# One table of expert slots for all four batches, filled in two passes, in a fused block of attention, mixture of experts and rotation

## The chip, the cores and the metric

The kernel runs on one core of one Trainium2 chip, in float32. Times are microseconds (us) of one execution on the device. A time without further words is the median of several runs; the profile is of one execution.

## The reference

Four batches of 512 tokens with 288 channels go through a block with adaptive layer norms, a mixture of experts, and then a rotation of a 64-dimensional subspace. Cut to what matters:

```python
mod = silu(c) @ w_adaln + b_adaln             # 6 vectors of 288 for each batch
h = ln(x) * (1 + sc_msa) + sh_msa
q, k, v = heads(h @ w_qkv + b_qkv)            # 16 heads of 18
o = softmax(q k^T * 18 ** -0.5) v
x = x + g_msa * (o @ w_proj + b_proj)
xn = ln(x) * (1 + sc_mlp) + sh_mlp            # 2048 tokens
logits = xn @ w_gate                          # 4 experts
gates = softmax(top2(logits))
eo[e] = gelu_tanh(xn @ w1[e] + b1[e]) @ w2[e] + b2[e]     # 288 -> 1152 -> 288
x = x + g_mlp * sum_e(gate[e] * eo[e])        # for a token's two experts
U, _ = qr(P)                                  # P is 288 x 64
R = expm(skew(silu(c) @ W.T + b))             # 64 x 64 for each batch
out = x + ((x U) R - x U) U^T
```

With two experts for each token there are 4096 rows of expert work. From the reference's inputs, the rows of the four experts are 229, 226, 337, 232 in batch 0; 193, 284, 265, 282 in batch 1; 177, 265, 297, 285 in batch 2; 249, 262, 281, 232 in batch 3.

## The kernel before

The whole order of instructions on each engine is written out by hand: the program is traced in the order in which its pieces are called, and no scheduler moves anything. All of it is in `fast_path`; another path, `general_path`, follows behind a flag and runs only if some expert gets more rows than its slots.

**Attention (to 270.6 us).** The work is cut into 32 pairs, eight for each batch (`HALF`): groups of four heads by pairs of token tiles. In a pair TensorE computes scores (`z`, L1905), ScalarE their exponentials (`es`, L1914, two for each group), and TensorE multiplies them with the values (`av`, L1925, in `gather`). The list `plan` places all other pieces into slots of the pairs, called a, s and b: projections of the next batch (`pq`, L1827; `pv`, L1790), the output projection of the batch before (`merges`, `po`, L1999), its routing (`choose`), columns of a Householder QR on VectorE (`column`, L1617 to L1693, one after another, 64 in all), the squarings of the matrix exponential (`square`, `psq`, L1514), the clearing of tables, and scatters (`scatter_next`, one indirect DMA on GpSimd for each tile of 128 tokens and each of its two choices, L2275). Normalized tiles `xh` are made by ScalarE (only batch 0's first norm by VectorE), transposed by TensorE and modulated into `hT` (L1250, L1256).

**Tables.** Batches are handled in two halves of two. In each half the experts are ranked by their rows, and rank r has `CAPS[r]` slots, in a table `slots0` or `slots1` of 2304 rows of 296 values: 288 channels, four weights and four places, each by rank. A row is scattered to its slot by its rank within its expert (`ranks_of`, pc L2155 to L2169, then `slots_of`). The sums go to `chosen0` and `chosen1`.

**Experts (270.6 to 630.2 us).** For each half and rank, eight times in all, i = 0 to 7:

- `hidden(i)`: 9 blocks f, taken by twos. For each block, matmuls of `w1s` (L2648) and of the last 32 channels from `w1r` (L2661) with the transposed slots `xgT` into `ph`; then ScalarE's gelu into `hm` (L2670).
- `outputs(i)`: tiles of 128 slots. For each, 18 matmuls into `pe` (L2708), a weighted sum `y`, and an indirect DMA on GpSimd that adds the rows to `chosen` (L2725). Each of these DMAs waits until the one before it has landed.
- Ranks 1 and 2 have 576 slots, which is four tiles and a half; their two halves form one shared tile, whose rows are in `xgS` and `hmS`, and which belongs to rank 2's outputs.
- `load_slots(i + 1)` (on SP; for i = 0 on GpSimd, during attention) and its transposes (`pt`, L2406, copied to `xgT` by ScalarE, L2407) lie between them, and the weights of the next expert are loaded on SP (`expert_weights`).

A list `rest` gives one more piece to each of 108 steps (72 blocks and 36 tiles): batch 2's routing, batch 3's merges and routing, the remaining columns, and at its end `ends`: the basis chain from `pwt` (L1698) over `pg`, `pnt`, `pN` and `pR` (L1725 to L1729) to `pY`, `pU` and `pu`, with the loads and additions of the first batches' sums beside it.

**Finish (630.2 us to the end).** `Finish` takes pairs of token tiles in turn: transposes (`pxT`, L2784), `pz` (L2795), `py` (L2810), an addition on VectorE (L2818) and a store (L2820).

The slots of a half in the kernel before:

```python
CAPS = (640, 576, 576, 512)
FIRST = (0, 640, 1216, 1792)
SLOTS = 2304
ROW = 288 + 2 * 4
```

Of the kernel before, what the change touches and what calls it, by code (L numbers as in the profile page):

```python
# [10 lines left out]
F32 = mybir.dt.float32  # L11
# [17 lines left out]
CAPS = (640, 576, 576, 512)  # L29
FIRST = (0, 640, 1216, 1792)  # L30
SLOTS = 2304
ROW = 288 + 2 * 4
# [3 lines left out]
WARM = 6  # L36
# [794 lines left out]
def fast_path(  # L831
# [76 lines left out]

    slots = [dram.tile([SLOTS, ROW], F32, name=f"slots{h}") for h in range(HALVES)]

    chosen = [
        dram.tile([B * N // HALVES, C], F32, name=f"chosen{h}")
        for h in range(HALVES)
    ]
# [3 lines left out]
    brow = [const.tile([P, E + 1], I32, name=f"brow{h}") for h in range(HALVES)]  # L918
    b1r = const.tile([P, HALVES, E, NF], F32, name="b1r")
    numbers, wxs = {}, []  # L920

    def expert_weights(i):
# [4 lines left out]
        h, r = divmod(i, E)  # L927
# [48 lines left out]
    with ExitStack() as s1:  # L976
# [78 lines left out]
        def compact(item, copy):  # L1055
            w = wqk[:CC, :, item, :].rearrange("p k (h d) -> p k h d", d=HD)
            for at, i, h, n in parts_of(item):
                heads = raws[int(h >= HS)].rearrange("p k t (h r) -> p k t h r", r=HQ)
                copy(w[:, :, ds(at, n), :], heads[:, :, i, ds(h - HS * (h >= HS), n), :HD])
            w = wqk[CC : CC + 1, 0, item, :].rearrange("o (h d) -> o h d", d=HD)  # L1060
            b = braw.rearrange("o (c r t g) -> o t g c r", c=4, t=2, g=NG)
            for at, i, g, c, n in in_groups(item):
                copy(w[:, ds(at, n), :], b[:, i, g, ds(c, n), :HD])
# [107 lines left out]
        bounds = const.tile([P, 2, E, E], F32, name="bounds")  # L1171
# [3 lines left out]
        for e in range(E):  # L1175
            nc.gpsimd.memset(bounds[:, 0, :, e : e + 1], float(FIRST[e]))
            nc.gpsimd.memset(bounds[:, 1, :, e : e + 1], float(FIRST[e] + CAPS[e]))
            nc.gpsimd.memset(expert[:, :, e : e + 1], float(e))
            nc.gpsimd.memset(ranks[:, e, :], float(e))
            nc.gpsimd.memset(tie[:, e : e + 1], float(E - 1 - e))  # L1180

        tokeni = const.tile([P, TT // HALVES], I32, name="tokeni")
        nc.gpsimd.iota(
            tokeni, pattern=[[P, TT // HALVES]], base=0, channel_multiplier=1
        )
        token = const.tile([P, TT // HALVES], F32, name="token")
# [6 lines left out]
        nc.gpsimd.memset(empty[:, :C], 0.0)  # L1193
        nc.gpsimd.memset(empty[:, C:], 1.0e6)
# [16 lines left out]

        def spreads_of(b, which, mv):
# [3 lines left out]
            if (b, which) != (0, 0):  # L1216
# [7 lines left out]
        def normalized(b, which, mv, rs):  # L1224

            xh = rt.tile([P, NT, C], F32, tag="xh", name=f"xh{which}{b}", bufs=2)
            for t in range(NT):
                if (b, which) != (0, 0):
# [4 lines left out]
                        bias=mv[:, t : t + 1],  # L1233
# [31 lines left out]
        def clear_slots():  # L1265
            def clear(h, i):
                nc.gpsimd.dma_start(out=slots[h][ts(i, P), :], in_=empty)

            def clear_sums(h, i):
                nc.sync.dma_start(  # L1270
                    out=chosen[h][ds(i * 4 * P, 4 * P), :].rearrange("(t p) c -> p t c", p=P),
                    in_=empty[:, :C].unsqueeze(1).to_broadcast([P, 4, C]),
                )

            return [
                lambda h=h, i=i: clear(h, i)
                for h in range(HALVES)
                for i in range(SLOTS // P)
            ] + [
                lambda h=h, i=i: clear_sums(h, i)  # L1280
                for h in range(HALVES)
                for i in range(B * N // HALVES // (4 * P))
            ]
# [66 lines left out]
        def skew_matrices(between):  # L1350
# [51 lines left out]
            def stores(part):  # L1402
                for at, (r, to, i, lo, n) in enumerate(runs[part::8]):
# [9 lines left out]
            def last():  # L1413
# [25 lines left out]
                + [lambda part=part: stores(part) for part in range(8)]  # L1439
                + [load]  # L1440
                + idle * 2
# [3 lines left out]
        def rotations():  # L1445
# [124 lines left out]
            def last():  # L1570
# [8 lines left out]
                + [lambda k=k: square(k) for k in range(SQUARINGS_FAST)]  # L1579
# [353 lines left out]
        def normalize(n):  # L1933
# [18 lines left out]
            def first():  # L1952
# [7 lines left out]
                for c, k, at in placed:  # L1960
                    (nc.gpsimd if n == NN - 1 else nc.sync).dma_start(out=chunk(oTs, k, "oc")[at, :], in_=oraw[ds(c * HQ, HD), :])
# [90 lines left out]
        TH = BH * NT  # L2052
        halves = {}
        scatters = []
        scattered = [[] for _ in range(HALVES)]
# [5 lines left out]
        def choose(b, xr):  # L2061

            h, b1 = divmod(b, BH)
            tiles = ds(b1 * NT, NT)
            if b1 == 0:
                halves[h] = (

                    small.tile([P, 2, TH, E], F32, tag="kk", name=f"kk{h}", bufs=2),  # L2070

                    small.tile([P, TH, 2, E], F32, tag="raw", name=f"raw{h}", bufs=2),

                    small.tile([P, TH, E], F32, tag="both", name=f"both{h}", bufs=2),
                    small.tile([P, TH + 1, E], F32, tag="sums", name=f"sums{h}", bufs=2),
                    [],
                )
            kk, raw, both, sums, xrs = halves[h]
            xrs.append(xr)
            k1, k2 = kk[:, 0, tiles, :], kk[:, 1, tiles, :]  # L2080
# [42 lines left out]
            def choices():  # L2123
                nc.vector.tensor_add(both[:, tiles, :], k1, k2)
                if b1 == 0:
                    nc.vector.memset(sums[:, 0, :], 0.0)
                for t in range(b1 * NT, (b1 + 1) * NT):
                    nc.vector.tensor_add(sums[:, t + 1, :], sums[:, t, :], both[:, t, :])

                nc.vector.tensor_copy(  # L2130
                    raw[:, tiles, 1, :],
                    token[:, tiles].unsqueeze(2).to_broadcast([P, NT, E]),
                )

            def gates_of():
# [6 lines left out]
                cb = raw[:, tiles, 0, :]  # L2142
# [8 lines left out]
            def ranks_of():  # L2151

                pc = bank([P, N], f"pc{h}")
                pn = pc[:, TH * E : (TH + 1) * E]
                nc.tensor.matmul(  # L2155
                    pc[:, : TH * E],
# [6 lines left out]
                    pc[:, : TH * E],  # L2163
                    every,
                    sums[:, :TH, :].rearrange("p t e -> p (t e)"),
# [3 lines left out]
                nc.tensor.matmul(pn, every, sums[:, TH, :], start=True, stop=True)  # L2169

                def square(name):
                    return small.tile([P, E, E], F32, tag=name, name=f"{name}{h}", bufs=1)


                pos = small.tile([P, TH + 1, E], F32, tag="pos", name=f"pos{h}", bufs=1)
                nc.vector.tensor_copy(
                    pos.rearrange("p t e -> p (t e)"), pc[:, : (TH + 1) * E]
                )
                size = small.tile([P, E], F32, tag="size", name=f"size{h}", bufs=1)
                nc.vector.scalar_tensor_tensor(  # L2180
                    size, pos[:, TH, :], float(E), tie, ALU.mult, ALU.add
# [10 lines left out]
                has = square("has")  # L2192
# [6 lines left out]
                for half in range(2):  # L2199
                    part = ts(half, P // 2)  # L2200
                    nc.vector.tensor_copy(
                        number[part, E : E + 1], number[part, half + 1 : half + 2]
                    )
                nc.vector.tensor_copy(brow[h], number)
                ends_ = small.tile([P, 2, E, E], F32, tag="ends", name=f"ends{h}", bufs=1)
                nc.vector.tensor_tensor(
                    ends_,
                    bounds,
                    has.rearrange("p r e -> p e r").unsqueeze(1).to_broadcast([P, 2, E, E]),
                    ALU.mult,  # L2210
                )
                first_last = small.tile([P, 2, E], F32, tag="fl", name=f"fl{h}", bufs=1)
                nc.vector.tensor_reduce(first_last, ends_, AX.X, ALU.add)
                nc.vector.tensor_copy(lastslot[:, h], first_last[:, 1])
                nc.vector.tensor_add(nextslot[:, h], first_last[:, 0], pos[:, TH, :])
                kept.extend((pos, has, first_last[:, 0]))

            def by_rank():

                has = kept[2]  # L2220
                of = small.tile([P, TH * 2, E, E], F32, tag="of", name=f"of{h}", bufs=1)
                nc.vector.tensor_tensor(
                    of,
                    raw.rearrange("p t k e -> p (t k) e")
                    .unsqueeze(2)
                    .to_broadcast([P, TH * 2, E, E]),
                    has.unsqueeze(1).to_broadcast([P, TH * 2, E, E]),
                    ALU.mult,
                )
                for i, xr_ in enumerate(xrs):  # L2230
                    nc.vector.tensor_reduce(
                        xr_[:, :, C:],
                        of[:, ds(i * NT * 2, NT * 2)].rearrange(
                            "p (t k) r e -> p t (k r) e", k=2
                        ),
                        AX.X,
                        ALU.add,
                    )
# [6 lines left out]
                    has.unsqueeze(2).to_broadcast([P, E, NF, E]),  # L2245
# [4 lines left out]
            def slots_of():  # L2250
                pos, _, firsts = kept[1:]
                pos = pos[:, :TH, :]

                def all_(m):
                    return m.unsqueeze(1).to_broadcast([P, TH, E])

                nc.vector.tensor_tensor(pos, pos, all_(firsts), ALU.add)

# [785 lines left out]
```

## Time and profile before

| | |
|---|---|
| runs of the kernel before | 659.48, 659.94, 659.95 us; median 659.94 |
| the profiled execution's own time | 658.79 us |
| its span (first to last instruction) | 657.1 us |
| granted TensorE clock | 0.996 of full speed |
| TensorE (PE) busy | 644.2 us, 98% |
| VectorE (DVE) busy | 440.9 us, 67% |
| ScalarE (ACT) busy | 293.7 us, 45% |
| GpSimd (POOL) busy | 267.1 us, 41% |

The expert stage in the profile begins at these times (us), hidden(i) first and then outputs(i):

| i | 0 | 1 | 2 | 3 | 4 | 5 | 6 | 7 |
|---|---|---|---|---|---|---|---|---|
| hidden | 270.6 | 324.4 | 366.4 | 411.4 | 451.1 | 498.4 | 539.8 | 587.2 |
| outputs | 299.4 | 346.8 | 387.9 | 431.1 | 474.8 | 520.2 | 561.3 | 612.7 |

How to read the views: the page's busy tenths cut the span into 40 slices, one digit each. The chain goes back from the last instruction to what released each, and is told in order of time as start, duration, engine, tile and line, with the number of instructions in a run. The timeline tells the same for one engine, with `[idle before <-releaser]` where the engine had stood idle. A matmul's end is modelled, so a group's duration is a little longer than its share of the engine, and periods are read from starts.

### The profile page before, as it was taken

The page shows a single profiled execution, that of the slowest core. Times are in us where ns is not written, and L with a number is a line of the kernel's source. Part 1 is how long each engine was busy: PE and PEld are TensorE (multiplying, and loading weights), DVE is VectorE, ACT ScalarE, POOL GpSimd, SP SyncE. Part 2 cuts the span into 40 slices and gives each one's busy share as a digit, 9 for nine tenths or more (in the row PEclk, how much of TensorE's full clock was granted, in tenths as well). Part 3 has the DMA queues.
Part 4 walks back from the last instruction along what each step waited for, and adds up shares of the span by engine and source line. Part 5 has one row for each costly group of instructions (what it writes and reads, how often), then busy time and mean ns, then how long its engine had stood idle before and what let it go on. Part 6 is the DMA issues. An engine that isn't in the chain of part 4 may idle for free.

```text
span 657.1 us, 11381 instructions
## 1 busy us (share of the span) xinstructions
PE 644.2 (98%) x3558; PEld 380.9 (58%) x3558; DVE 440.9 (67%) x1989; ACT 293.7 (45%) x469; POOL 267.1 (41%) x392
## 2 busy tenths in 40 slices
PE   7999999999999999999999999999999999999995
PEld 3534344443444344567767767776677676776763
DVE  5545757796667137582989988888888898342125
ACT  4468557775686557743343232232323322312232
POOL 4034589754352766503505745314043042251120
PEclk9999999999999999999999999999999999999998
DMA  8549333232323644366416642665064353551044
GB/s 211 117 149 231 111 87 94 81 110 73 106 72 86 196 137 112 118 178 181 76 16 208 141 156 38 160 181 91 17 173 82 92 126 58 135 123 34 10 84 159
DMA packets 77364, 75.74 MB, mean 115 GB/s; under 512 B 35168, under 2 KB 67437, under 8 KB 77294
## 3 DMA queue, kind: packets, MB, share of 16 engines
q1 hardware_dynamic: 62106, 47.88, 26.6%
q0 software_dynamic: 14784, 26.62, 17.6%
q8 instruction: 30, 0.49, 0.3%
q10 hardware_dynamic: 404, 0.42, 0.3%
q14 instruction: 40, 0.33, 0.2%
HBM read 47.68 MB, written 20.88 MB: 104 GB/s over the span
## 4 chain that ended last, share of the span: by engine, by line
PE 88%; DMA 5%; DVE 3%; SPq 2%; ACT 1%; issue 1%; DVEq 0%; ACTq 0%
PE pe L2708 24%; PE ph L2648 22%; PE z L1905 9%; PE av L1925 7%; PE pq L1827 6%; PE ph L2661 4%; PE po L1999 4%; PE pv L1790 3%; PE pt L2406 2%; DMA raw<-in_w_qk_dram 1%; PE pz L2795 1%; PE pxT L2784 1%; DMA qk<-row 1%; DMA rdr<-den 1%; DVE pl L2088 1%; PE py L2810 1%
## 5 line engine op out<-in xcount | busy, mean ns | idle before, releaser
L2708 PE MATMUL pe<-w2s,hm 128*128 128x288 f32 (+1 forms) x648 | 163.7, 408 | 0.0
L1914 ACT ACTIVATE es<-z 128x1024 f32<-128x1024 f32 x128 | 126.3, 1023 | 64.3 <-PE z L1905 62.2
L2648 PE MATMUL ph<-xgT,w1s 128*128 128x288 f32 (+2 forms) x576 | 151.7, 413 | 0.4
L2708 PEld LDWEIGHTS pe<-w2s,hm 128*128 128x128 f32 (+1 forms) x648 | 118.7, 187 | 31.8 <-issue 2.3
L2648 PEld LDWEIGHTS ph<-xgT,w1s 128*128 128x128 f32 x576 | 105.8, 190 | 40.6 <-issue 11.9
L2670 ACT ACTIVATE hm<-ph,b1r 128x576 f32<-128x576 f32 (+2 forms) x72 | 49.9, 738 | 122.0 <-PE ph L2661 122.0
L2725 POOL DMA_INDIRECT chosen<-y,place x38 | 61.0, 1604 | 69.4 <-DMA chosen<-y,place 36.9
L1905 PE MATMUL z<-qk 32*128 32x512 f32 x512 | 78.4, 639 | 0.2 <-DMA qk<-row 0.2
L2723 POOL TENSOR_TENSOR y<-y,gb 128x288 f32<-128x288 f32 x32 | 27.9, 872 | 115.6 <-ACT y L2722 115.6
L2722 ACT ACTIVATE y<-pe,weight 128x288 f32<-128x288 f32 x32 | 16.0, 501 | 107.3 <-PE pe L2708 107.3
L1925 PE MATMUL av<-es,vt 128*32 128x512 f32 x512 | 61.7, 598 | 0.0
L1827 PE MATMUL pq<-hT,wqk 96*126 96x512 f32 (+4 forms) x156 | 59.0, 510 | 1.2 <-ACT hT L1256 1.2
L1827 PEld LDWEIGHTS pq<-hT,wqk 97*126 97x126 f32 (+3 forms) x156 | 25.5, 178 | 38.3 <-issue 30.1
L2275 POOL DMA_INDIRECT slots<-xr,where x32 | 32.5, 1014 | 35.1 <-DVE where L2272 21.1
L1646 DVE STREAM_SHUFFLE wj<-pt 32x288 f32<-32x288 f32 (+47 forms) x96 | 42.2, 439 | 0.6
L1905 PEld LDWEIGHTS z<-qk 32*128 32x128 f32 x512 | 23.5, 182 | 26.8 <-ACT es L1914 16.8
L1925 PEld LDWEIGHTS av<-es,vt 128*32 128x32 f32 x512 | 13.5, 109 | 42.8 <-issue 42.8
L1874 POOL DMA_DIRECT2D qk<-row x42 | 21.2, 510 | 40.8 <-ACT row L1869 30.8
L1620 DVE SCALAR_TENSOR_TENSOR pt<-wj,uf,pt 64x288 f32<-64x288 f32 (+62 forms) x63 | 34.5, 548 | 2.2
L1635 DVE SCALAR_TENSOR_TENSOR q<-q 64x1 f32<-64x1 f32 (+1 forms) x128 | 31.0, 242 | 4.6
L1617 DVE SCALAR_TENSOR_TENSOR prf<-pt,q,wj 64x288 f32<-64x288 f32 (+62 forms) x63 | 31.6, 501 | 2.2
L2661 PE MATMUL ph<-xgT,w1r 32*128 32x288 f32 (+2 forms) x288 | 30.6, 453 | 0.0
(286 smaller groups left out, 826.6 us busy)
## 6 DMA issues: line engine op xcount, KB each, us to landing
w2s<-in_w_dram SPq DMA_DIRECT2D x8, 1296.0 KB
w1s<-in_w_dram SPq DMA_DIRECT2D x8, 1152.0 KB
slots<-empty POOLq DMA_DIRECT2D x36, 148.0 KB, 3.2
qk<-row POOLq DMA_DIRECT2D x42, 72.0 KB, 3.3
spread<-rdr SPq DMA_DIRECT2D x64, 36.0 KB
chosen<-empty SPq DMA_DIRECT2D x4, 576.0 KB
out_dram<-xs SPq DMA_DIRECT2D x8, 288.0 KB
wr<-in_wrT_dram POOLq DMA_DIRECT2D x4, 567.0 KB, 5.2
```

The source lines that it names most:

```text
L1620: nc.vector.scalar_tensor_tensor(m, w, u[rows, :], m, ALU.mult, ALU.add)
L1646: nc.vector.stream_shuffle(wj[o : o + HQ, j:], pt[o0 : o0 + HQ, j:], [j % HQ] * HQ)
L1827: nc.tensor.matmul(pq[:n, at], wqk[:rows, k, item, :n], hT[:rows, k, at], start=start, stop=(k == NK - 1),)
L1905: nc.tensor.matmul(zs[c // 2][:, c % 2, :], qk[ts(c, HQ), 1, ts(t, P)], qk[ts(c, HQ), 0, :], start=True, stop=True,)
L1914: nc.scalar.activation(e, z, AF.Exp, scale=SCALE)
L1925: nc.tensor.matmul(avs[n][ts(c, HQ), :], vts[b % 2][:, t, ds((4 * g + c) * (HD + 1), HQ)], es[c // 2][:, c % 2, :], start=(t == 0), stop=( ...
L2275: made = nc.gpsimd.indirect_dma_start(out=slots[h], out_offset=bass.IndirectOffsetOnAxis(ap=where[:, i, t : t + 1], axis=0), in_=xrs[t // ...
L2648: nc.tensor.matmul(ph[:, j, :SB], w1s[:, k, ts(f, P)], xgT[:, k, ts(j, SB)], start=(k == 0), stop=False,)
L2661: nc.tensor.matmul(ph[:, j, :SB], w1r[rows, f0 // 2, :], xgT[rows, 2, ts(j, SB)], start=False, stop=True,)
L2670: nc.scalar.activation(hm[:, f, : CAPS[r]].rearrange("p (j s) -> p j s", j=NB), ph[:, :, :SB], AF.Gelu_apprx_tanh, bias=b1r[:, h, r, f : f ...
L2708: nc.tensor.matmul(po[ts(m, rows), :], slots_[:, f, :], w[:, f, :], start=(f == 0), stop=(f == NF - 1),)
L2725: nc.gpsimd.indirect_dma_start(out=chosen[h], out_offset=bass.IndirectOffsetOnAxis(ap=place[:, t + m : t + m + 1], axis=0), in_=y, in_offs ...
```

## The change

- There is one table `slots` with 1280 rows for each expert, of 293 values (288 channels, four weights by expert, one place), and one `chosen`. Positions run on over all four batches. The first pass is ranked after batches 0 and 1 and has 640, 576, 544 and 512 slots; rows of batch 2 fill what is free in it, except for the biggest expert, whose batch-2 rows begin at its 640th slot. The second pass takes what is left, with 640, 576, 448 and 512 slots, where the third expert worked on is rank 3 (448) and the fourth is rank 2 (512). By the counts above the second pass has 578, 493, 455 and 336 rows.
- `load_slots` starts at rows read into registers, with two DMAs in place of six; GpSimd then copies the last 32 channels three times more (`copies`) and picks the weights (`ends`). The second expert's load is issued behind the first hidden layer and waits for batch 2's scatters.
- There are 35 output tiles in place of 36.
- Batch 2's normalized tiles are made by VectorE. Its norm, logits and choices move from the first hidden layer into pairs 29 to 31, its last two merges share pair 28, and three columns leave the attention stage for the expert stage.
- The tables are cleared from pair 6 on, `chosen` in eight DMAs of 288 KB, each behind a reciprocal of batches 1 to 3 (it was four of 576 KB). The skew matrices are stored in seven parts, and `square(0)` gets a step without work behind it.
- At the front there is one warm-up group fewer, two of batch 0's normalized tiles are made by ScalarE, and the second half of the query and key weights is compacted by VectorE.
- At the end the basis chain takes the last 13 of 111 steps, from the last hidden layer on; an output tile of the last expert counts as two steps. The check of the flag comes behind it, and the last store is two of one tile each.

The core of the diff:

```diff
-CAPS = (640, 576, 576, 512)
-FIRST = (0, 640, 1216, 1792)
-SLOTS = 2304
-ROW = 288 + 2 * 4
+CAPS = ((640, 576, 544, 512), (640, 576, 448, 512))
+ORDER = ((0, 1, 2, 3), (0, 1, 3, 2))
+STRIDE = 1280
+SLOTS = 4 * STRIDE
+ROW = 288 + 4 + 1
...
-WARM = 6
+WARM = 5
...
+        PLAIN = ((0, 0), (B - 2, 1))
...
-                if (b, which) != (0, 0):
+                if (b, which) not in PLAIN or (b == 0 and t >= NT // 2):
                     nc.scalar.activation(
...
-            def clear_sums(h, i):
+            def clear_sums(i):
                 nc.sync.dma_start(
-                    out=chosen[h][ds(i * 4 * P, 4 * P), :].rearrange("(t p) c -> p t c", p=P),
-                    in_=empty[:, :C].unsqueeze(1).to_broadcast([P, 4, C]),
+                    out=chosen[ds(i * 2 * P, 2 * P), :].rearrange("(t p) c -> p t c", p=P),
+                    in_=empty[:, :C].unsqueeze(1).to_broadcast([P, 2, C]),
...
+                at = begun[:, b] if b else firsts
+                nc.vector.tensor_tensor(
+                    pos,
+                    pc[:, : (NT + 1) * E].rearrange("p (t e) -> p t e", e=E),
+                    at.unsqueeze(1).to_broadcast([P, NT + 1, E]),
+                    ALU.add,
+                )
...
+            load(xg[:, :n], ds(at, n * P), lambda m: m.rearrange("(t p) c -> p t c", p=P))
...
+            def copies():
+                nc.gpsimd.tensor_copy(
+                    xg[:, :n, C : 3 * P].rearrange("p t (g c) -> p t g c", c=HQ),
+                    xg[:, :n, 2 * P : C].unsqueeze(2).to_broadcast([P, n, 3, HQ]),
                 )
...
+            if n >= NG:
+                clear(1, 1)
...
                     for t, piece in enumerate(merges):
-                        also(at + 2 + t, "s", piece)
+                        also(at + 2 + min(t, 2), "s", piece)
                     routes[b - 1] = routing(b - 1)
+                    also(at + 5, "s", routes[b - 1][0])
+                    also(at + 5, "b", routes[b - 1][1])
+                    also(at + 6, "s", routes[b - 1][2])
+                    also(at + 7, "s", routes[b - 1][3], routes[b - 1][4])
...
-            SB = CAPS[r] // NB
+            SB = CAPS[h][u] // NB
...
-                for t in range(5 if r == 0 else 4)
+                for t in range(own_tiles(h, u))
...
+                    if f == NF // 2 and i + 1 == HALVES * E:
+                        yield
...
+            if not i:
+
+                takes = take_slots(1, load_slots(1, hp, "xg", 1))
```

## The prediction

> **What bounds the kernel now.** I read the page first: engine totals, the busy tenths, and the chain that ended last. Then came the chain entry by entry, and the timelines of the places that the diff touches.
>
> ```profile
> PE 644.2 (98%) x3558; PEld 380.9 (58%) x3558; DVE 440.9 (67%) x1989; ACT 293.7 (45%) x469; POOL 267.1 (41%) x392
> PE   7999999999999999999999999999999999999995
> DVE  5545757796667137582989988888888898342125
> ...
> PE 88%; DMA 5%; DVE 3%; SPq 2%; ACT 1%; issue 1%; DVEq 0%; ACTq 0%
> ```
>
> TensorE is busy for 644.2 of 657.1 us and full in every slice but the first and the last. VectorE is at 80 to 90% in the expert stage until 562.9 us. So TensorE work that goes away is time won, unless another engine is then late for it; VectorE is the nearest.
>
> **The change part by part.** The profiled execution took 658.79 us (span 657.1), 1.15 below the median of the runs, 659.94. The sum is made on the profiled one.
>
> *Narrower hidden layers.* Two blocks f of the hidden layer are 16 matmuls against w1s, and repeat as the chain shows:
>
> ```profile
> 375.54 4.08 PE ph L2648 x16
> 380.32 4.08 PE ph L2648 x16
> ...
> 415.70 3.65 PE ph L2648 x16
> 419.99 3.65 PE ph L2648 x16
> ...
> 461.17 4.50 PE ph L2648 x16
> 466.42 4.50 PE ph L2648 x16
> ```
>
> The periods are 4.78 us for 576 slots, 4.29 for 512, 5.25 for 640, so about 0.48 us for every 64 slots. A layer has 4.5 such steps, so 64 slots cost 2.15 us. The cap goes from 576 to 544 in the first pass (-1.08) and from 576 to 448 in the second (-4.30): -5.4. Below 512 slots no row shows a period. With no gain there it would be -3.2; I take the line: 3.65 us over 16 is 0.228 for 256 columns, the line gives 0.20 for 224, and the weight loads beside these matmuls take 0.19 each by the page.
>
> *One output tile and one transposed tile fewer.*
>
> ```profile
> 612.72 17.66 PE pe L2708 x72
> ```
>
> Four tiles of 18 matmuls take 17.66 us, so a tile takes 4.42. The second pass's third layer has four tiles in place of five: -4.4. The transposes of a tile and their wait are worth 0.3: -0.3.
>
> *Positions for two more batches.* They are worked once for each batch, no longer once for two: four groups of matmuls in place of two, each like the one from 208.82 to 209.51 us (pc), 0.69: +1.4.
>
> *The end of attention.* Batch 2's merges now lie in pairs 26, 27, 28 and 28, no longer in 29, and its routing in 29 to 31.
>
> ```profile
> 254.02 1.51 PE L1905 MATMUL z<-qk 32*128 32x512 f32 x8
> 255.46 1.73 PE L1999 MATMUL po<-wpg,oc 108*128 108x288 f32 x6
> ```
>
> Pairs 28 to 31 take 6.14, 6.20, 6.14 and 4.2 us. With two merges pair 28 should take 6.0 + 1.66 = 7.66; 29 and 30 are held near 6.1 by ScalarE's two 1.02-us exponentials for each group of scores and can't shrink; pair 31, with batch 2's logits, 4.9: +2.1 (0 if the po hides in waits for the exponentials, +3 if the logits wait for VectorE's norm, four passes of about 0.4 us). The routing leaves a first hidden layer in which TensorE never waits (28.80 us busy of 28.80) and is about 1 us of its work there; that small gain is left in the range.
>
> *Slot loads.* Two DMAs in place of six, then copies by GpSimd. The first load starts behind batch 2's rs at about 255.4 us, after a register load; landing about 262 and the copies 1 to 1.3 us (nearest row: a 576-element GpSimd copy, 0.70), against a need at 266: hidden, with 3 us to spare, and 1 us for each one that it is late. The later loads sit on SP behind the same releases as before, with the weights of the next expert behind them. Transposed tiles are placed earlier in the output layers: copies that were bare in two places and are now bare in one other: +0.5.
>
> *Clearing in smaller pieces.* At 234.26 TensorE waits 0.88 us for XY, which stands on VectorE behind the spread of reciprocals, whose DMA queues on SP behind a 576-KB clear of `chosen`:
>
> ```profile
> 210.26 5.25 DMA chosen<-empty
> ...
> 234.26 0.68 PE L1514 MATMUL psq<-XY 64*64 64x64 f32 x16 [0.88 <-DVE XY L1568]
> ```
>
> The clears become eight of 288 KB, each behind a reciprocal's own DMAs, and square gets an idle step: -0.9 (0 if a clear falls elsewhere in the way). The four more `slots` clears are on GpSimd's queue in attention and hidden.
>
> *Front.*
>
> ```profile
> 12.62 0.51 ACT L1059 COPY wqk<-raw 96x378 f32<-96x378 f32 x1 [1.18 <-DMA raw<-in_w_qk_dram]
> ...
> 13.67 2.11 ACT L1256 ACTIVATE hT<-pt,modT 96x512 f32<-96x512 f32 x3
> ...
> 14.59 5.39 PE L1827 MATMUL pq<-hT,wqk 97*126 97x512 f32 x12 [1.22 <-ACT hT L1256]
> ```
>
> hT stands on ScalarE behind the compaction of the second weight half. That copy goes to VectorE, its biases to GpSimd, one warm-up group goes away, and ScalarE gets two normalized tiles earlier, while it is idle. pq should start near 13.4: -1.2 (0 if the weights, which land at 12.60, then wait for VectorE).
>
> *End.* The basis chain, from pwt to pU, moves from the last two layers into the second half of the last hidden layer and the last output layer; each of its steps has 8 to 10 matmuls (1.96 to 2.4 us) over a VectorE answer of 0.28 to 0.71 us. The last store becomes two of one tile: -0.5 (0 to -0.8, half a tile pair of VectorE and half a transfer).
>
> Sum: -5.4 - 4.4 - 0.3 + 1.4 + 2.1 + 0.5 - 0.9 - 1.2 - 0.5 = -8.7 us. Span 648.4, profiled time 650.1, median about 651.3.
>
> **The rivals.** First, *VectorE's column chain becomes the bound*. The 64 columns of the QR are worked one after another on VectorE, and TensorE needs the last at pwt.
>
> ```profile
> 346.88 0.45 DVE L1646 STREAM_SHUFFLE wj<-pt 32x269 f32<-32x269 f32 x1
> ...
> 558.59 0.40 DVE L1646 STREAM_SHUFFLE wj<-pt 32x225 f32<-32x225 f32 x1
> ...
> 566.10 0.37 PE L1698 MATMUL pwt<-ident,pt 64*96 64x64 f32 x3
> ```
>
> The chain ended at 562.9, 3 us ahead of pwt. The twelve columns from 346.88 to 411.82 average 5.41 us, the 33 after them 4.58. The change takes three columns out of attention, so 48 remain, from about 350.5: 15 x 5.41 + 33 x 4.58 = 232.3, ending at 582.8. The last hidden layer began at 587.2 and begins 10.2 earlier (the sum without the last store, -8.2, and 2 us of chain that move behind it), at 577.0; pwt stands two periods (8.6) and half a step (2.0) into it, so at about 587.6. That leaves 5 us. For: GpSimd gets seven copies and some thirty small products in this stage, and VectorE's small steps do stretch beside it:
>
> ```profile
> 273.19 0.62 DVE L1678 SCALAR_TENSOR_TENSOR kap<-q 64x1 f32<-64x1 f32 x1
> 273.84 0.72 DVE L1681 TENSOR_TENSOR q<-kap,behind 64x1 f32<-64x1 f32 x1
> ...
> 273.71 2.52 POOL L1994 TENSOR_TENSOR wpg<-wp,gates 108x288 f32<-108x288 f32 x3
> ```
>
> Both usually take 0.15 us. Against: seven times 1.3 us plus thirty times 0.1 is 12 us, of which VectorE loses perhaps a third, 4 us, just inside the 5. [...] Worked from the rows alone: 1 us is lost for each us after 587.6. With late columns at 4.85 the end is 591.7, +4.1, and the median 655.4. It gets slower than before when the late columns average over 5.0; at 5.05 (+0.47 x 33 = 15.5 us) the end is 598.3, 10.7 late, and the median 662.
>
> Second, *batch 2's scatters hold the second expert's load*. Its rows now lie in the first pass, so the load waits for eight more scatters at about 1.6 us each after batch 2's positions at about 281, and lands near 305, needed at 317. GpSimd's queue also holds the products and copies there. If it lands late, each us is lost, and the weights behind it on SP (needed at 324) follow. 5 us late gives about 656.
>
> Third, *less gain*: no gain below 512 slots, +3 at the end of attention, no gain at the front: -8.7 + 2.2 + 0.9 + 1.2 = -4.4, so 655.5. And the change may not do what it says: rows that don't fit would run the other path, at far more than the time now. From the reference's inputs the remainders of the second pass are 578, 493, 455 and 336 against 640, 576, 512 and 448, so they fit.
>
> **How the numbers follow.** The forecast, nothing new late, has 0.62: 651.3, with 648 to 654.5 by its terms. The column chain late has 0.18, 0.11 of it at 653 to 658.6; the load late 0.08, the smaller gain 0.11, the fallback 0.01. The range is 647 to 658: below, the terms at their good ends; above, the chain about 7 us late. A measurement of this kernel can tell about 0.2%, 1.3 us. Slower by more, over 661.3: 0.05 of the chain's, 0.02 of the load's and the fallback, 0.08. Within: 0.04, the chain's 0.02 and the load's 0.02. Faster: the rest, 0.88.
>
> **What would show it.** In the changed profile: periods of about 4.5 and 3.8 us for 544 and 448 slots; four tiles of 18 matmuls in the second pass's third layer; pq near 13.4; no wait at psq; pairs 28 to 31 about 2 us longer; last columns ending 3 to 6 us before pwt, and no idle time ahead of pwt; transposes of the second expert without a wait for the load. It is wrong if pwt, or the second expert's first transposes, follow idle time of several us, if attention ends over 4 us later than before, or if TensorE's busy time is not about 8 us shorter.

## The result

The changed kernel takes 654.48 us (median of 17 runs, 651.23 to 660.87) against 660.34 for the kernel before in the same runs. The ratio is 0.9907, with a 95% interval of 0.9887 to 0.9927: about 6 us faster. The prediction said 651.3, in a range of 647 to 658. The direction was right, and so was the mechanism in the main; 3 us of the 8.7 are missing in the median. Ratios leave out the few executions that fell in a slower state of the chip, while the medians of the experiments count them (three of twelve in e2_merges, 663.6 to 664.7 us at clocks of 0.985 to 0.990).

The profiled execution took 655.60 us, its span 654.0 (before: 658.79 and 657.1). So in the profiles 3.1 us are gained, 5.6 fewer than summed. The page of the changed kernel:

```profile
PE 637.9 (98%) x3547; PEld 377.4 (58%) x3547; DVE 443.1 (68%) x2016; ACT 285.3 (44%) x446; POOL 275.0 (42%) x432
PE   8999999999999999999999999999999999999995
...
PEclk9999999899999999899999999999999999999998
...
PE 93%; DMA 3%; ACT 1%; DVE 0%; POOL 0%; issue 0%; SPq 0%; DVEq 0%; ACTq 0%
```

TensorE's busy time fell by 6.3 us. But the row of the granted clock, full until the last slice before, now has two eights in the middle, and TensorE's waits are others than before (engine, line, releaser; us in total, times, longest):

```profile
PE pm L1106 <- DVE qk L1073: 2.6, 1, 2.6
PE z L1919 <- ACT es L1928: 1.6, 2, 0.8
PE ptA L1431 <- DMA um<-udr: 1.4, 1, 1.4
PE pq L1841 <- ACT hT L1274: 0.6, 1, 0.6
PE pv L1804 <- DMA wv<-in_w_v_dram: 0.6, 1, 0.6
```

The first was there before, and pq's was 1.2. The others are new (`um` is the skew matrices read back from memory for the exponential, which `ptA` transposes), and the timeline shows what comes behind two of them:

```profile
122.05 2.70 PE L1804 MATMUL pv<-wv,hT 96*128 96x288 f32 x10
126.12 0.91 PE L1431 MATMUL ptA<-ident,um 64*64 64x64 f32 x8 [1.38 <-DMA um<-udr]
126.96 2.09 PE L1919 MATMUL z<-qk 32*128 32x512 f32 x8
...
264.52 2.04 PE L1919 MATMUL z<-qk 32*128 32x512 f32 x8 [0.80 <-ACT es L1928]
266.50 3.62 PE L1939 MATMUL av<-es,vt 128*32 128x512 f32 x16
```

Eight z take 1.14 us in the pairs before and at 126.96 2.09; sixteen av take 1.92 and at 266.50 3.62. The stretches of 1 us around both places (PE, PEld, DVE, ACT and POOL busy, then the granted clock, the DMA share and GB/s):

```profile
125.00:126.00 1.00, 0.00 (x0) 0.00 (x0) 0.97 (x3) 1.00 (x3) 0.00 (x0) 1.00 0.42 123
126.00:127.00 1.00, 0.88 (x12) 0.62 (x12) 0.96 (x3) 0.80 (x3) 0.00 (x0) 0.80 0.05 5
127.00:128.00 1.00, 1.00 (x9) 0.48 (x8) 1.00 (x6) 0.00 (x0) 0.00 (x0) 0.50 0.05 4
...
129.00:130.00 1.00, 1.00 (x12) 0.34 (x12) 1.00 (x7) 0.85 (x1) 0.00 (x0) 0.50 0.15 37
130.00:131.00 1.00, 1.00 (x16) 0.16 (x8) 0.80 (x5) 0.53 (x2) 0.11 (x4) 0.99 0.25 64
...
266.00:267.00 1.00, 1.00 (x8) 0.20 (x8) 1.00 (x3) 0.78 (x1) 0.92 (x2) 0.78 0.44 58
267.00:268.00 1.00, 1.00 (x8) 0.22 (x4) 1.00 (x3) 0.00 (x0) 1.00 (x2) 0.50 0.05 11
```

From 126.60 to 130.01 TensorE ran at half clock, 3.41 us, which costs 1.7; the same again from 266.55 to 269.96. No step of the prediction had that.

### The profile page after: what moved, and what is told of

Same layout as the page of the kernel before. It is cut to its first block, busy times and chain, and to the rows that moved or that the text cites. A ratio compares the mean times of both kernels' runs of the same rounds, so it can differ in the third digit from the quotient of the medians.

```text
span 654.0 us, 11451 instructions
## 1 busy us (share of the span) xinstructions
PE 637.9 (98%) x3547; PEld 377.4 (58%) x3547; DVE 443.1 (68%) x2016; ACT 285.3 (44%) x446; POOL 275.0 (42%) x432
## 4 chain that ended last, share of the span: by engine, by line
PE 93%; DMA 3%; ACT 1%; DVE 0%; POOL 0%; issue 0%; SPq 0%; DVEq 0%; ACTq 0%
PE pe L2782 24%; PE ph L2720 22%; PE z L1919 11%; PE av L1939 9%; PE pq L1841 8%; PE ph L2733 4%; PE po L2015 4%; PE pv L1804 3%; DMA wv<-in_w_v_dram 2%; PE pt L2465 1%; PE pz L2896 1%; PE pxT L2885 1%; PE py L2918 1%; PE psq L1527 1%; DMA xs<-in_x_dram 1%; DMA slots<-empty 0%
## 5 line engine op out<-in xcount | busy, mean ns | idle before, releaser
L2782 PE MATMUL pe<-w2s,hm 128*128 128x288 f32 (+1 forms) x630 | 160.6, 409 | 0.0
L2720 PE MATMUL ph<-xgT,w1s 128*128 128x320 f32 (+4 forms) x576 | 146.6, 404 | 0.6 <-ACT xgT L2466 0.4
L2782 PEld LDWEIGHTS pe<-w2s,hm 128*128 128x128 f32 (+1 forms) x630 | 114.9, 187 | 31.1 <-issue 3.1
L2742 ACT ACTIVATE hm<-ph,b1r 128x640 f32<-128x640 f32 (+4 forms) x72 | 48.6, 720 | 119.0 <-PE ph L2733 119.0
L2799 POOL DMA_INDIRECT chosen<-y,place x37 | 59.0, 1595 | 71.4 <-DMA chosen<-y,place 30.2
L2797 POOL TENSOR_TENSOR y<-y,gb 128x288 f32<-128x288 f32 x31 | 26.2, 847 | 94.9 <-ACT y L2796 94.8
L1939 PE MATMUL av<-es,vt 128*32 128x512 f32 x512 | 63.9, 617 | 0.0
L1634 DVE SCALAR_TENSOR_TENSOR pt<-wj,uf,pt 64x288 f32<-64x288 f32 (+62 forms) x63 | 30.9, 490 | 2.2
L2733 PE MATMUL ph<-xgT,w1r 32*128 32x320 f32 (+4 forms) x288 | 29.9, 445 | 0.0
```

The source lines that it names most:

```text
L1939: nc.tensor.matmul(avs[n][ts(c, HQ), :], vts[b % 2][:, t, ds((4 * g + c) * (HD + 1), HQ)], es[c // 2][:, c % 2, :], start=(t == 0), stop=( ...
L2720: nc.tensor.matmul(ph[:, j, :SB], w1s[:, k, ts(f, P)], xgT[:, k, ts(j, SB)], start=(k == 0), stop=False,)
L2733: nc.tensor.matmul(ph[:, j, :SB], w1r[rows, f0 // 2, :], xgT[rows, 2, ts(j, SB)], start=False, stop=True,)
L2742: nc.scalar.activation(hm[:, f, : CAPS[h][u]].rearrange("p (j s) -> p j s", j=NB), ph[:, :, :SB], AF.Gelu_apprx_tanh, bias=b1r[:, h, r, f ...
L2782: nc.tensor.matmul(po[ts(m, rows), :], slots_[:, f, :], w[:, f, :], start=(f == 0), stop=(f == NF - 1),)
L2799: made = nc.gpsimd.indirect_dma_start(out=chosen, out_offset=bass.IndirectOffsetOnAxis(ap=place[:, t + m : t + m + 1], axis=0), in_=y, in_ ...
```

## The experiments

Unless another base is named, an edit is one to the changed kernel. The runs fell on several chips, so ratios to the kernel before, run beside each, are compared.

**The slots.**

```diff
-CAPS = ((640, 576, 544, 512), (640, 576, 448, 512))
-ORDER = ((0, 1, 2, 3), (0, 1, 3, 2))
+CAPS = ((640, 576, 576, 512), (640, 576, 576, 512))
+ORDER = ((0, 1, 2, 3), (0, 1, 2, 3))
```

> The changed kernel with the caps of before: 576 slots in the third place of both passes and ranks worked in order, 36 output tiles; one table and all else as changed. If the slots are where the gain comes from, as the sum has it (5.4 us of hidden layer, 4.4 us of output tile, 0.3 of transposes), this is 10 us slower than the changed kernel, about 664 against 654, which is slower than before; periods of two blocks 4.78 us in both third layers. The rival, that narrower layers only move the wait elsewhere: under 6 us slower.

663.39 us, ratio 1.0032 (1.0006 to 1.0057): with the old caps the new table makes the kernel slower than before. Ratio against ratio it is 8.3 us slower than the changed kernel, and 10.9 at the shortest runs of both (662.11 and 651.23). The chain of the changed kernel has the periods that the line gave for 544 and 448 slots:

```profile
376.02 3.86 PE ph L2720 x16
380.56 3.86 PE ph L2720 x16
...
546.83 3.22 PE ph L2720 x16
550.64 3.23 PE ph L2720 x16
```

4.54 and 3.81 us, against 4.5 and 3.8. The gain of the change is the slots; all else in it together costs.

**The fourth merge back in pair 29.**

```diff
-                        also(at + 2 + min(t, 2), "s", piece)
+                        also(at + 2 + t, "s", piece)
```

> The changed kernel with batch 2's fourth merge back in pair 29, so that a merge lies between the scores of that pair. Theory: the changed kernel loses 0.80 us of TensorE twice ahead of scores in pairs 29 and 30, and behind that the granted clock is 0.50 for 3.7 us, worth 1.8 us. With the merge back the wait of pair 29 is gone, pair 28 is 1.6 us shorter and pair 29 1 us longer; if the low clock needs both waits, it is gone too: 0.8 to 2.5 us faster than the changed kernel, mean clock up by 0.002. Rival, that the low clock comes from something else (the load of the table at that time, 1.0 of the DMA share): 0.8 us at most and the low clock stays.

657.27 us, ratio 0.9934 (0.9906 to 0.9963): not faster. The wait of 0.80 in pair 29 is gone; the one in pair 30 stays, and no low clock follows it. But batch 2's choices then come late on VectorE, and its positions in the first hidden layer wait 2.63 us, with half clock from 279.7 to 283.2 behind that:

```profile
278.13 0.37 PE L2151 MATMUL pc<-both,below 128*128 128x16 f32 x2 [2.63 <-DVE sums L2125]
```

So the merge in pair 28 buys that wait off. Neither expectation had it.

**Clears out of um's way.** No clears of slots behind pairs 9 to 13, five in a pair later; the clear of chosen at n = 5 left to a later group.

```diff
-            if n >= NG:
+            if n >= NG and n != NG + 1:
                 clear(1, 1)
...
-            if pair >= HALF - 2:
-                clear(0, 2 if pair < 2 * HALF else 3 if pair < 3 * HALF - 4 else 4)
+            if pair >= HALF - 2 and not 9 <= pair <= 13:
+                clear(0, 3 if pair < 2 * HALF else 5)
```

> The changed kernel without clears of slots behind pairs 9 to 13 and without the clear of chosen behind the sixth group's reciprocals (they come behind other pairs). Theory: the DMA um<-udr came late because SyncE waited 4.6 us for rdr<-den, which shared the DMA engines with slots<-empty, and then issued a 288-KB clear ahead of it. Then ptA's wait of 1.38 us is gone, and with it the 3.7 us at clock 0.50 behind it (1.8 us): 3 us faster than the changed kernel. Rival, that the seven parts of the skew stores make um late: the wait stays at over 1 us.

655.71 us, ratio 0.9926 (0.9895 to 0.9956). The wait at ptA and the low clock behind it are gone. The 3 us are not won: 1.43 us at pw (a product of the exponential) and 0.77 at po stand in the profile, and the low clock behind pair 30 stays. On SyncE's queue `rdr` stores the reciprocals of a group's softmax sums and `spread` reads them back; behind them come a clear of `chosen` and `um`. The queue in the changed kernel, then in this run:

```profile
116.68 0.94 SPq L1982 DMA_DIRECT2D rdr<-den  x1
121.26 1.35 SPq L1986 DMA_DIRECT2D spread<-rdr  x4
...
123.42 1.18 SPq L1424 DMA_DIRECT2D um<-udr  x2
```
```profile
117.87 0.35 SPq L1982 DMA_DIRECT2D rdr<-den  x1
119.90 1.35 SPq L1986 DMA_DIRECT2D spread<-rdr  x4
121.29 0.39 SPq L1288 DMA_DIRECT2D chosen<-empty  x1
122.06 1.18 SPq L1424 DMA_DIRECT2D um<-udr  x2
```

The clear of `chosen` ahead of um is still there; the edit moved the one after it. What changed is that rdr, issued as late as before, has no `slots` clears beside it and is followed by spread after 2.0 us, not 4.6. But one profile of each would not show it, since the wait comes and goes with the clears in place. All eleven other profiles have a burst of four `slots` clears there. In seven of them, the changed kernel's first among them, rdr is issued 2.4 to 3.8 us after the burst begins, spread follows 3.2 to 4.6 us later, and ptA waits 0.2 to 1.38 us in all. In four (e1_caps, e6_one_store, e8_busy_again, and e11_after, which is the changed kernel again) rdr is issued before the burst or level with it, spread follows after 1.4 to 1.5 us, and ptA does not wait. So the clears hold um up when they win this race. The wait at pw is no price of the edit: e11_after has 1.77 us there.

**Useless work in the waits.** The test that tells the clock from the lateness:

```diff
+        def busy_work():
+            nothing = bank([P, N], "nothing")
+            for _ in range(8):
+                nc.tensor.transpose(nothing[:, :P], ident, ident)
...
+                also(at + 5, "s", busy_work)
+                also(at + 6, "s", busy_work)
```

> The changed kernel with eight transposes of the identity, read by nobody, ahead of the second scores of pairs 29 and 30, to fill TensorE's two waits of 0.80 us there; about 1 us of useless work each. Theory of the clock: the low clock behind pair 30 comes from TensorE's waits and not from the lateness itself, so it goes away with useless work: 1 to 2 us faster than the changed kernel although it works more. Rival, that the exponentials alone set these pairs and the clock has another cause: same time or up to 0.5 us slower, and the low clock stays.

652.27 us, ratio 0.9887 (0.9841 to 0.9934), against 0.9907 without. The intervals overlap, so the profiles have to decide. The timeline in pair 30:

```profile
262.48 1.09 PE L2546 MATMUL nothing<-ident 128*128 128x128 f32 x8
263.50 1.89 PE L1919 MATMUL z<-qk 32*128 32x512 f32 x8
265.32 1.92 PE L1939 MATMUL av<-es,vt 128*32 128x512 f32 x16
```

The av take 1.92 us again, the clock is full until the finish, and the pairs are not longer: 6.21 us from pair to pair against 6.20. From the av of pair 29 to the first expert it is 13.0 us against 14.7. The useless work costs nothing, since ScalarE's exponentials set these pairs and TensorE has the time. One profile would not settle the clock, because e11_after has both waits, full clock behind them and the same 13.0 us. All together do: half clock follows pair 30 in three of the four profiles with both waits (the changed kernel, e1_caps and e3_quiet, not e11_after), and in none of the seven with the useless work.

**Useless work with fewer clears in the way.** e4_busy, with clears from pair 4 on but none behind pairs 11 and 12.

> The changed kernel with the useless transposes of e4_busy, and with clears of slots from pair 4 on but none behind pairs 11 and 12, and no clear of chosen behind the sixth group's reciprocals; later pairs clear as in the changed kernel, unlike e3_quiet. Theory: ptA's wait (1.38 us in the changed kernel, 0.66 in e4_busy) is gone and no other takes its place: 0.5 to 1.5 us faster than e4_busy, near 651.5 and, with the clock kept, less spread over the runs. Rival, that any clear moved makes another small transfer late: another wait of about 1 us appears in attention and the time is that of e4_busy.

On a chip where the kernel before took 668.99 us this took 654.83, ratio 0.9803 (0.9761 to 0.9845), the lowest ratio of its set, beside 0.9824 (0.9770 to 0.9877) for e4_busy there: not told apart. ptA waits 0.20 us; the burst of four clears ahead of rdr is still there. The profile has 1.62 us ahead of z at 41 us, on qk<-row, with half clock from 40.7 to 47.6; e6_one_store, whose clears start two pairs later, has 1.80 us in the same place, so the clears don't make it. There no half clock follows.

**One last store.** e4_busy, the last store in one piece.

> e4_busy with the last store as it was before, one of two tiles behind one addition. My sum had the split at -0.5 us, so without it +0.5. The profiles say otherwise: from the end of the last matmul to the end of the span it is 6.4 us in the kernel before and 7.2, 6.9 and 6.4 in three kernels with two stores, so I now expect -0.4 us, with 6.4 us behind the last matmul.

655.71 us, ratio 0.9839 (0.9787 to 0.9891): against e4_busy's 0.9824 the time can't tell. The profiles can. From the end of the last matmul to the end of the span it is 6.4, 6.6 and 6.7 us in three kernels with one store, and 6.4 to 7.8, nine of ten above 7, with two. (No trace has the 6.9 of the expectation: e1_caps, e2_merges and e3_quiet have 7.5 to 7.8.)

**Twelve waits of set length.** e4_busy, with a wait after every fourth or fifth step or so of the expert stage.

```diff
...
+        def wait_for(widths):
+            first, then = bank([P, N], "first"), bank([P, N], "then")
+            nc.tensor.transpose(first[:, :P], ident, ident)
+            nc.scalar.copy(lag[:, :P], first[:, :P])
+            for width in widths:
+                nc.scalar.copy(lag[:, :width], lag[:, :width])
+            nc.tensor.transpose(then[:, :P], lag[:, :P], ident)
...
```

> e4_busy with twelve waits of TensorE put into the expert stage, where it is otherwise full: one transpose, a copy by ScalarE, none to two more copies of 256 to 960 elements, and a transpose that reads them; lengths from about 0.5 to 2.5 us, four of them twice. Output and all else unchanged. It asks from which length a wait costs the clock. If a wait of 0.8 us is enough by itself, at least nine of the twelve are followed by 3.4 us at clock 0.50, 1.7 us each, and the time is 15 us of waits and 15 us of clock above e4_busy. If it takes more than half of a window of 3.4 us, only the two or three longest are. If it depends on where the wait lies in a window, equal waits come out differently.

681.10 us (two runs). The waits came out at 0.36 to 2.92 us, 19.8 in all, and only two were followed by half clock. Four of them:

```profile
421.06 0.33 PE L3038 MATMUL then<-ident,lag 128*128 128x128 f32 x1 [2.03 <-ACT lag L3037]
...
477.29 0.47 PE L3038 MATMUL then<-ident,lag 128*128 128x128 f32 x1 [2.92 <-ACT lag L3037]
...
495.59 0.33 PE L3038 MATMUL then<-ident,lag 128*128 128x128 f32 x1 [2.83 <-ACT lag L3037]
...
572.64 0.33 PE L3038 MATMUL then<-ident,lag 128*128 128x128 f32 x1 [2.08 <-ACT lag L3037]
```

Half clock follows the first (from 422.3) and the second (from 476.9), not the third and fourth. The two beginnings are 54.6 us apart, 16 x 3.41, the length of a stretch of half clock in the changed kernel's profile; there 126.6 and 266.6 are 140.0 apart, 41 x 3.41. So the beginnings of a profile stand on a grid of 3.41 us. The half clock that ends every profile, behind the last matmul, begins on it too: in the changed kernel's at 648.8, 112 x 3.413 us behind 266.6. All nine beginnings of half clock before the finish, in seven profiles, lie a whole number of windows of this grid (58 to 179) ahead of the one at its end, so I lay out the windows of every profile from there.

The 2.03 us lay whole in one window, 60% of it; the 2.83 were cut by a window's edge into 1.2 and 1.6, and the 2.08 left 1.9 in one. Equal waits do come out differently. What decides in attention is not settled, where narrower matmuls fill the rest. At pw 1.59 us in one window were enough (e10_best), and 1.52 (e11_after) and 1.43 (e3_quiet) were not; 1.38 were enough at ptA. Of the waits of 0.80 us, the one in pair 30 was followed by half clock in three of five profiles. The one in pair 29 never was, although it too lay whole in one window in the same three.

**The base of those three again.**

> e4_busy once more, as the base of the three others and for a narrower interval: 652.3 us again, 2 us below the changed kernel.

655.34 us where the kernel before took 668.99: ratio 0.9824 (0.9770 to 0.9877). Its profile's span is 649.6 us, full clock until the finish. The changed kernel did not run on that chip, so the 2 us are not measured here.

**Whole tiles at the end.** e4_busy, without the extra step at `f == NF // 2`.

> e4_busy without the halving of the last expert's output tiles: they are four steps and no longer eight, so the basis chain, still the last 13 steps, begins four steps earlier, in the first block of the last hidden layer. Two things are tested. First the price of a late column chain (the rival of the prediction): pwt stands at about 578.8 us where the columns end at 584 to 585, so TensorE should wait 5 to 6 us there, 1 us for 1 us. Second the halves: a halved tile is two groups of 2.14 and 2.62 us where a whole one is 4.37, so whole tiles should save 4 x 0.4 = 1.6 us. Together 3.5 to 4.5 us slower than e4_busy, plus up to 3.4 us if the clock is lost behind the wait. If the column chain had more slack than I read, it is faster than e4_busy by 1 to 1.6 us.

657.49 us, ratio 0.9916 (0.9884 to 0.9949).

```profile
583.36 0.34 PE L1712 MATMUL pwt<-ident,pt 64*96 64x64 f32 x3 [2.65 <-DVE pt L1707]
```

TensorE waits for the columns, as the rival had it; no half clock follows, and a window's edge cuts the 2.65 us into 1.9 and 0.75. The last hidden layer and outputs take 48.6 us, 2.3 more than in e4_busy; without the 2.65 of the wait they would take 45.9, so halving the tiles costs 0.4 us, not 1.6. The wait was half as long as expected, because the columns ended 4.8 us into the last hidden layer, and 8.0 in e4_busy's profile.

**What helped, in one**: e5_quiet_busy with the single store, and **the changed kernel beside it.**

> What helped, in one: the useless transposes of e4_busy, the clears of e5_quiet_busy, the single last store of e6_one_store. Expected 3 us below the changed kernel run beside it (2 from the clock, 0.7 from um, 0.5 from the store), and the fastest of all.

> The changed kernel itself, beside the two others on the same chip. Expected at 0.990 of the kernel before, as measured; in its profile a low clock behind pairs 29 and 30 again, and a wait of 0.6 to 1.4 us at ptA.

652.97 us, ratio 0.9863 (0.9838 to 0.9888), against 655.72, ratio 0.9918 (0.9887 to 0.9949), for the changed kernel: 2.75 us by the medians, with intervals that just touch. It is the fastest of the three kernels tried on that chip. Its profile is of its longest run (span 654.4): ptA waits twice, 0.30 and 0.39 us, and behind 1.59 us at pw there is half clock from 179.3 to 182.7. The changed kernel's second profile (span 652.5) missed what was expected of it. It has 1.77 us at pw, no wait at ptA, both waits of 0.80 us ahead of z, and full clock throughout:

```profile
176.25 0.45 PE L1527 MATMUL pw<-pw,An 64*64 64x64 f32 x8 [1.77 <-DVE xs L2034]
...
264.31 2.04 PE L1919 MATMUL z<-qk 32*128 32x512 f32 x8 [0.80 <-ACT es L1928]
266.28 1.93 PE L1939 MATMUL av<-es,vt 128*32 128x512 f32 x16
```

The program and the waits in pairs 29 and 30 are those of the first profile; what was seen to differ is their place in the grid. So the loss behind a wait is a chance, and the spread of the 17 runs goes with it: those of mean clock 0.995 and above took 651.2 to 654.5 us, the one of 0.986 took 660.9.

## Why the prediction was right, and where its sum was off

**Right.** The hidden layers (-5.4): the third of the first pass took 22.23 us and takes 21.17, -1.06; of the second 22.23 and 17.44, -4.79, 0.5 better than the line. The step from 512 to 448 slots, for which no row spoke, held. The output tile: outputs of the second pass's third layer fell by 6.7 us, 4.4 and 0.3 as summed and the 2.0 of the basis chain that left it. Pairs 28 to 31: 24.5 us without the low clock against 22.7, +1.8 of +2.1. The wait at psq is gone. The second rival did not come: the second expert's transposes begin at 318.88 with no idle time before them.

Two of the prediction's own signs of being wrong did come in the first profile. Attention ended 4.5 us later (275.06 against 270.57), over the 4 that it allowed, and TensorE's busy time fell by 6.3 us, not about 8. Both stretches of half clock (1.7 us each) and ptA's wait lie in attention, and half clock makes busy time longer too: sixteen av took 3.62 us in place of 1.92. In e11_after, without them, attention ends at 273.15 and the busy time is 636.1 us, 8.1 less than before.

**The rival, VectorE's columns.** 48 columns from 354.97 (the sum had 350.5) took 4.77 us each; the sum had 4.84. They ended at 584.0 (predicted 582.8), and pwt did not wait:

```profile
583.77 0.22 DVE L1707 TENSOR_TENSOR pt<-pt,tri 64x64 f32<-64x64 f32 x1
```
```profile
590.49 0.37 PE L1712 MATMUL pwt<-ident,pt 64*96 64x64 f32 x3
```

The late 33, on which the price hung, took 4.60 us each, against 4.58 before. The slack is 6.5 us here and 6.0 in e11_after, where 5 was forecast; it is 2.8 in e4_busy, e6_one_store and e8_busy_again, whose columns take about 4.85 us each, and why they do is not shown. So the rival was near, and with its price: e9_whole_tiles put pwt ahead of the columns' end and paid. No run shows the columns 7 us late, as at the upper end of the forecast's range: pwt comes 6.5 and 6.0 us behind their end in the two profiles of the changed kernel, and the wait in e9_whole_tiles is 2.65. What GpSimd's work beside VectorE's came to, the trace shows at a copy:

```profile
550.36 0.51 POOL L2422 COPY xg<-xg 128x384 f32<-128x384 f32 x1
```
```profile
550.42 0.48 DVE L1692 SCALAR_TENSOR_TENSOR kap<-q 32x1 f32<-32x1 f32 x1
```

The step, 0.15 us at its median, takes 0.48 and ends with the copy, 0.33 late. The seven copies of this stage take 0.43 to 1.17 us, 4.5 together where I had put 9.1, and 23 small products 5.6 where I had put 3. So GpSimd's 10 us were near the 12, but they were not lost to the chain: its late columns are hardly slower than before.

**Off.** The step that failed is "Clearing in smaller pieces": "The four more `slots` clears are on GpSimd's queue in attention and hidden", and its -0.9, which was to be 0 "if a clear falls elsewhere in the way". The clears were costed by the queue that issues them, and by the one late transfer that they were known to cause. In the profiled execution a burst of them lay ahead of a small transfer, rdr; spread, which waits for it, was issued 4.6 us after it, so spread, the clear of chosen and um came late on SyncE, and ptA waited 1.38 us. Psq's 0.9 were won, and 1.4 lost there. Since the same program did not wait at ptA in its second profile, this is a loss of some executions and not of all; what it costs in the median is not measured.

Missing altogether is the clock: 1.7 us behind that wait and 1.7 behind pair 30, where "held near 6.1 by ScalarE's two 1.02-us exponentials" was right but took a wait of TensorE to cost only its length. That is 3.4 of the 5.6 in this profile; in e11_after, without it, 4.6 us are gained by the spans, 4.1 fewer than summed, 1.77 of them at pw.

Smaller ones: "End" was costed at nothing for the chain and is 1.2 us longer on TensorE over the last three stages, 0.4 of it by the halved tiles (e9_whole_tiles); the rest I can't place. The last store cost about 0.8 in the profile instead of gaining 0.5. The front's -1.2 shows at pq (13.43 us, said 13.4) but is 0.3 at the first scores, because the values' weights land at 19.4 and pv waits 0.58 for them; 1.3 more came at 40 us, where a wait for qk<-row was absent in this profile, which two others have again with 1.6 and 1.8 us.

## What to carry to other kernels

On a path that one engine fills to 98%, work taken away was won (here within half a us of what was summed), and it could be costed from the periods in the chain. But a wait of that engine can have a second price, here half clock for 3.41 us (6.9 in e5_quiet_busy) in nine places of seven profiles, 1.7 us lost for each 3.41; so filling an unavoidable wait with useless matmuls can be worth it: half clock followed pair 30 in three of the four profiles with both waits, and in none of the seven with the useless work. And a bulk transfer cut in pieces and spread out was not hidden by its queue: ptA waited 0.2 to 1.38 us in the seven profiles where rdr was issued behind a burst of clears. Look at which small transfers with a waiter are in flight beside it.

## What I had not expected of the hardware

- TensorE ran at half clock for 3.41 us behind waits that are far shorter than that: 0.80 and 1.38 us in attention, 2.03 among full matmuls (where 1.9 in one window were not enough). The edges lie on a grid of 3.41 us that does not begin with the kernel: counted back from the beginnings of half clock, its first edge is 0.3 us behind the first instruction in the changed kernel's profile, 1.8 in e10_best's and 2.5 in e7_waits'. The same wait in the same program, 0.80 us ahead of z in pair 30, cost 1.7 us in one execution and nothing in the next (e11_after). In the windows ahead of half clock TensorE was busy for 0.9 to 2.6 of 3.41 us; in others it was busy for as little (1.5 around the wait of 2.08 us in e7_waits, 2.6 in pair 29 of the changed kernel), and no half clock followed.
- Two stores of one tile ended later behind the last matmul (7.7 us at the median of ten profiles) than one of two tiles (6.4 to 6.7 in three).
